# The next pair's token reads split from their layernorm, two weight reads on another queue, filler matmuls and differences placed earlier

## The chip, the cores and the metric

One core of one Trainium2 chip runs the kernel: a whole decoder layer, one launch. The metric is the device time in microseconds (us). The core's engines are called PE (TensorE, matrix products), DVE (VectorE), ACT (ScalarE), POOL (GpSimd) and SP (SyncE, which here only issues transfers). Each engine works through its own list of instructions in order.

## What is computed

Three stages, each with a residual, on 2 batches of 2048 tokens of width 512, all in float32:

```
x = x + linear_attention(layernorm(x))          # 16 heads of 32, 128 features
x = x + cross_attention(layernorm(x), ctx)      # 154 keys a batch, 16 heads
x = x + experts(layernorm(x))

def experts(h):                                 # h: 4096 tokens x 512
    scores = softmax(h @ router_w, axis=-1)     # 8 experts
    topk_w, topk_idx = top_k(scores, 6)
    f_all = (silu(h @ w_gate) * (h @ w_up)) @ w_down       # for each expert, 256 wide
    y = sum(picked(f_all, topk_idx) * topk_w)
    return y + (silu(h @ ws_gate) * (h @ ws_up)) @ ws_down # shared, 512 wide
```

## The kernel before

The tokens are cut into 8 blocks of 512, and a block into 4 tiles of 128 (NT). Linear attention takes the time to about 640 us, cross attention to about 1090 us, and the experts run from about 1042 us to the end. Every float32 product is made of three matmuls of rounded parts: an operand is split into a high part (a cast on ACT) and a low part (the subtraction `low`, L118, on DVE or POOL).

**The experts.** Blocks go in pairs: pair 0 (blocks 0 and 1) to pair 3. Each pair passes ten units: the 8 experts and the two halves of the shared product. That makes 40 steps, `todo3`, numbered n = 0 to 39; u is the unit in a pair. A unit's up and gate products for two blocks and two halves of the width are made by a scheme of seven products (NP = 7, as in Strassen's), the parts s = 0 to 6 of `products(n)` (matmuls `pg`, L1092). Their left operands `wq{n}_{j}` are made from the raw weights in pair 0 (`prepare`, from `rgu`, with `low` and with sums on POOL or DVE) and stored to DRAM as `wqs`; later pairs read them back. Their right operands `xo{g}_{s}` are the tokens of the pair and four differences of them, a to d: `token_difference` (L1054, on POOL for every pair but the first) and then `tokens_part`, which splits into high and low (cast L1067 and L118). The results are combined on DVE (L1106, L1109, L1112, L1124). The down products are plain in pair 0 (`down`: matmuls `pf` L148, then accumulated on DVE at L1285, scaled by the gate), and again by seven parts in later pairs (`down_products`: `pf` L1205 from `ht` and `hb`, summed on DVE at L1226; between the two POOL multiplies with the gate rows `gr` (L1155) and makes differences (L1165 to L1168)).

**The tokens of the next pair.** While units 1 to 7 of a pair run, `normalize_ahead(b, t)` reads one tile of the next pair's two blocks (`xsn`, 256 KB, L287), makes its layernorm (statistics L245, `mv_n` L248, on POOL two small operations L250 and L251, and the application L252) and stores it again, to `xn2`. It is recorded at part s == 3, one tile a unit, and in unit 5 another at s == 6. In unit 8 (`expert_ahead`) these tiles are read back (`xsf`), transposed on PE (`ptf`) and copied to `raws`; then `route` and what follows it make the gates, and `store_gates` writes them to DRAM (`gated`, two stores). For pair 0, `expert_ahead` makes the layernorm itself, during the last block of cross attention.

**Order.** Work is recorded by generators that wait in a list, `dense`; each step of it records one matmul, and `dense.after(n, do)` records a piece n matmuls later. What is recorded is then put in order, engine by engine, by a scheduler that runs when the program is built, with costs of its own. An instruction recorded with `tc.keep_in_program_order` (called `held` in the code) may not pass the one recorded before it on its engine. All matmuls are held, the differences on POOL too (L1054), and the layernorm's statistics where `normalize(..., pinned=True)` is called (L245); everything else may be moved by the scheduler, transfers included. `places` says at which part of a pair's last unit (keys 0 to 6) and of the next pair's first unit (7 and up, that is NP + s) the next pair's differences and operands are recorded: `places[0]` for the steps from pair 1 to 2 and from 2 to 3 (n = 19 to 20 and n = 29 to 30), `places[1]` for the step from pair 0 to 1.

**Buffers.** Prepared weights, operands and raw weights share 17 buffers of 8 KB a partition (`eight`); work tiles of 2 KB share 9 (`half`); the token tiles `xsn` and `xsf`, cross attention's residual rows `xr_x` and the gate rows `gr` share five (tag `xs`). PSUM has four banks for `ps` (`pg` among others) and four for `sc` (`pf`, `ptf`, `pto`, `pgt`).

**The last block of cross attention.** At its second step the layernorm of block 0 is recorded, and `load_unit(0)` reads unit 0's raw weights (`rgu0`, two transfers of 512 KB, and `rd0`, one) on SP's queue. At its tenth step the layernorm and the transposes of block 1 (`ln`, `tr`), the first two products of unit 0 (`ready[0]`, `ready[1]`) and the last two output products of block 6 (`outs[2]`, `outs[3]`: `cross_out`, 12 matmuls `po_x` each) are put in line.

Of the kernel before, what the change touches and what calls it, by code (L numbers as in the profile page):

```python
# [24 lines left out]
NT = TB // P  # L25
# [12 lines left out]
def decoder_layer(  # L38
# [26 lines left out]
    nc = tc.nc  # L65
# [26 lines left out]
    def chunked(w):  # L92
        return w.rearrange("(c p) n -> p c n", p=P)
# [124 lines left out]
    dense = Dense()  # L218
# [66 lines left out]
    def load_tile(d, b, t, name):  # L285
        xs = work.tile([P, D], F32, tag="xs", name=f"xs{name}{b}_{t}", bufs=5)
        nc.sync.dma_start(out=xs, in_=tile_of(d, b, t))  # L287
        return xs
# [30 lines left out]
    x2 = [dram.tile([TB, D], F32, name=f"x2_{b}") for b in range(nblk)]  # L319
# [4 lines left out]
    xs = [half(f"xs{t}") for t in range(NT)]  # L324
# [6 lines left out]
    raw = wk  # L331
    wk = [eight([P, NC, D], FR, f"wk_{i}") for i in ("hi", "lo")]
    for t in range(NT):
# [5 lines left out]
        b = nc.vector.tensor_tensor(lo, pt, hi.bitcast(F32), ALU.subtract)  # L339
# [427 lines left out]
    for s in range(ws_gate.shape[1] // F):  # L767
# [9 lines left out]
        out=before,  # L777
        in_=before,
# [3 lines left out]
        base=0,  # L782
        channel_multiplier=0,
    )
    accs, raws, gates = {}, {}, {}
    xn2 = {b: dram.tile([TB, D], F32, name=f"xn2_{b}") for b in range(GROUP, nblk)}

    def expert_ahead(b):
# [22 lines left out]

        return [values(t) for t in range(NT)], [turn(t) for t in range(NT)]

    def normalize_ahead(b, t):

        xs = normalize(load_tile(x2[b], 0, t, f"n{b}_"), f"n{b}_{t}")
        dense.after(8, lambda: nc.sync.dma_start(out=tile_of(xn2[b], 0, t), in_=xs))
        yield from ()

# [112 lines left out]
    def load_unit(n):  # L932
        if n >= len(units):
            return
        g, up, dn, _ = units[n]
        raw = eight([P, 2, NC, F], F32, f"rgu{n}")
        nc.sync.dma_start(out=raw[:, 0], in_=chunked(g))
        nc.sync.dma_start(out=raw[:, 1], in_=chunked(up))
        if n:
            rawd = late.tile([P, NF, D], F32, tag="rd", name=f"rd{n}", bufs=1)  # L940
        else:
            rawd = eight([P, NF, D], F32, f"rd{n}")
        nc.sync.dma_start(out=rawd, in_=chunked(dn))
        wraw[n] = raw, rawd

    def summed(a, b, op, name, shape, eager):
# [453 lines left out]
    for n in range(len(steps) + LAG + 1):  # L1400
        if n < len(steps):
            b, c, t = steps[n]
            k = NT * c + t
            dense.until(xsts, (b, c))
            scores(b, c, t)
            if b == 0:
                if k == 0:
                    load_values(0)
                if k in (NC - 1 + 0, NC + 1 + 0):
                    load_reciprocals(nblk - 1, k - 0 - NC + 1)  # L1410
                if NC + 0 <= k < 2 * NC + 0:
                    attended(nblk - 1, k - NC - 0)
                if k == 8:
                    bor = load_row(bo, "bor")
                    xwo = split_weight(wo_t, "xwo")
            if b == 0 and k == 0:
                ln, tr = layernorm(x1[1], 1, 0, qts, "x")
                outs = [[attention_out(nblk - i, t) for t in range(NT)] for i in (2, 1)]
                new = [cross_query(1, i) for i in range(NC)]
                kinds = {"L": ln, "a": outs[0], "T": tr, "b": outs[1], "q": new}  # L1420
                dense.add(*(kinds[x].pop(0) for x in "LLLaTLTaTTaaqbqbqbqb"))
            if k == LAG + 0 and b:
                outs = [cross_out(b - 1, i) for i in range(NT)]
                new = [cross_query(b + 1, i) for i in range(NC)]
                if b + 1 < nblk:
                    ln, tr = layernorm(x1[b + 1], b + 1, 0, qts, "x")
                    kinds = {"L": ln, "o": outs, "T": tr, "q": new}
                    dense.add(*(kinds[x].pop(0) for x in "LLLoTLTTToqoqoqq"))
                else:
                    dense.add(outs[0], tr[0], ln[3], outs[1], *tr[1:])  # L1430
            if b == nblk - 1 and k == 1:
                ln, tr = expert_ahead(0)
                dense.add(*ln[:3])
                load_unit(0)
            if b == nblk - 1 and k == 9:
                ln, tr = expert_ahead(1)
                ready = products(0)
                dense.add(prepare(0, 0), *ln[:3], tokens_part(0, 0), tokens_part(0, 1))
                dense.add(tr[0], ready[0], ln[3], *tr[1:], ready[1], *outs[2:])
            dense.fill(fl(k, 9.5 if b == 0 else 7.75 if b < nblk - 1 else 5.5))  # L1440
            if b % bpb == bpb - 1 and b + 1 < nblk and c > 0 and t == 1:
                load_keys(b // bpb + 1, c - 1)
            if b % bpb == 0 and b and k == 0:
                load_keys(b // bpb, NC - 1)
        if LAG <= n < len(steps) + LAG:
            turn(*steps[n - LAG])
        if n > LAG:
            b, c, t = steps[n - LAG - 1]
            if t == NT - 1:
                values(b, c)  # L1450
                if c == NC - 1 and (b + 1) % bpb == 0 and b + 1 < nblk:
                    load_values((b + 1) // bpb)
# [28 lines left out]
    def load_until(n, kind, j, more):  # L1481
# [12 lines left out]


    places = [
        {1: "0", 3: "a1", 4: "b", 5: "c2d", 7: "3", 8: "4", 9: "5", 10: "6"},
        {1: "0", 2: "1", 3: "abc2", 4: "d3", 5: "4", 6: "5", 7: "6"},
    ]
    MORE = 3  # L1500
    for n, (group, u) in enumerate(todo3):
        early_group = n < len(units)
        g = group[0]
        more = group[-1] + 1 < nblk
        ahead = [[], []]
        if u == len(units) - 2 and more:
            ahead = [expert_ahead(b) for b in range(group[-1] + 1, group[-1] + 3)]
        parts = products(n) if n else ready
        downs = [[] for _ in range(NP)]
        if n > len(units):  # L1510
            downs = [[d] for d in down_products(n - 1)]
        if u == 1 and n > len(units) + 1:
            f0, f1 = finished(g - GROUP, 0), finished(g - GROUP, 1)
            downs[0] = f0[:2] + downs[0] + f0[2:]
            downs[1] = f1[:2] + downs[1] + f1[2:]
        if n == LAST:
            f0, f1 = finished(g, 0), finished(g, 1)
            d = downs
            downs = [d[0], d[1], d[2], d[3] + d[4], d[5] + d[6], f0, f1]
        for s, part in enumerate(parts):  # L1520
            if not early_group:
                if s % 2 == 0:
                    dense.add(load_until(n, "w", s // 2, MORE))
            if n or s > 2:
                dense.add(part)
            if not early_group:
                if s in (0, 4):
                    dense.add(load_until(n, "d", s // 4, MORE))
                dense.add(*downs[s])
            if u == len(units) - 1 and more and s in places[early_group]:  # L1530
                dense.add(*tokens_parts(group[-1] + 1, places[early_group][s]))
            if u == 0 and n and NP + s in places[n == len(units)]:
                dense.add(*tokens_parts(g, places[n == len(units)][NP + s]))
            if not n and s == 0:
                dense.add(prepare(0, 2), *(tokens_part(0, i) for i in (4, 5, 6)), prepare(0, 3))
            if not n and s == 5:
                dense.add(down_sums(0))
            if s == 1 and n and n <= len(units):
                dense.add(down(n - 1, 1))
            if s == 1 and not n:  # L1540
                dense.add(load_accs(group))
            at = u - 1 if s == 3 else NT + 2 if s == 6 and u == 5 else -1
            at += s == 3 and u > 6
            if more and 0 <= at < GROUP * NT and u < len(units) - 2:
                dense.add(normalize_ahead(group[-1] + 1 + at // NT, at % NT))
            if ahead[0]:
                (ln, tr), (ln2, tr2) = ahead
                todo = (ln, [], tr[:2], tr[2:] + ln2, [], tr2[:2], tr2[2:])
                dense.add(*todo[s])
            if s % 2 and n + 1 < len(units):  # L1550
                dense.add(prepare(n + 1, s // 2))
            if s == 5 and n + 1 == len(units):
                dense.add(load_until(n + 1, "w", 0, MORE))
        if n + 1 < len(units):
            dense.add(prepare(n + 1, 3), down_sums(n + 1))
        if early_group:
            dense.add(down(n, 0))
        if not n:
            load_unit(1)
        dense.run()  # L1560
        load_gates(n + 1)
        load_unit(n + 2)
# [73 lines left out]
```

## Time and profile before

| | us |
|---|---|
| median of 3 runs | 2323.12 (2322.77 to 2324.95) |
| the profiled execution | 2323.05 |
| its span, first to last instruction | 2321.2 |
| mean granted TensorE clock | 0.988 |

The granted clock is the share of full speed that the chip's throttle let TensorE have.

Busy time of the engines by stage:

```profile
core 0: us, PE busy (x) PEld busy (x) DVE busy (x) ACT busy (x) POOL busy (x), PEclk, DMA share, GB/s
0.00:640.00 640.00, 602.59 (x3917) 434.30 (x3918) 383.16 (x603) 387.68 (x706) 308.05 (x298) 0.98 0.75 218
640.00:1042.00 402.00, 378.84 (x2439) 289.05 (x2439) 299.34 (x688) 274.71 (x1132) 234.22 (x243) 0.98 0.62 179
1042.00:1404.00 362.00, 349.09 (x1580) 273.39 (x1578) 285.40 (x398) 156.22 (x295) 206.64 (x173) 0.99 0.64 235
1404.00:1694.00 290.00, 289.46 (x1289) 235.89 (x1290) 224.05 (x335) 92.27 (x155) 145.95 (x117) 1.00 0.60 228
1694.00:1999.00 305.00, 301.97 (x1359) 245.91 (x1358) 245.52 (x361) 99.30 (x162) 169.42 (x131) 0.99 0.61 230
1999.00:2321.00 322.00, 314.82 (x1400) 255.54 (x1398) 244.05 (x353) 90.98 (x150) 164.18 (x119) 1.00 0.55 204
```

A row is a stretch of the span: its start and end, its length, and then for PE, PE's weight loads, DVE, ACT and POOL the busy time in us with the number of instructions; then the granted clock, the busy share of the 16 DMA engines and what they moved. The rows are linear attention, cross attention up to the first expert product, and pairs 0, 1, 2 and 3. In a timeline line, further on, the columns are start, busy time, engine, line, operation, the tiles (output <- inputs), shapes and count, and in brackets the idle time of the engine before it and what ended that. PE's busy time is from modelled ends of matmuls that overlap; a matmul of 512 columns counts 0.39 us alone, and one follows another after some 0.23 us.

### The profile page before, as it was taken

To read this page: it belongs to the slowest core of one execution; us is meant where nothing else is said; L and a number is where in the kernel's file an instruction comes from. 1 tells how busy PE (TensorE), PEld (TensorE's weight loads), DVE (VectorE), ACT (ScalarE), POOL (GpSimd) and SP (SyncE) were. 2 spreads that over 40 slices of the span, in tenths; PEclk is the share of its full clock that TensorE was granted. 3 is DMA by queue.
4 is the path that set the end of the run, shared out by engine and by line. 5 is a ranking of instruction groups with operands and counts; after the bars stand their busy time and mean duration, and the time that the engine had idled before them with its cause. 6 is when DMAs were issued, how large, how long until landed. Compare 5 with 4: busy or idle time off the path is not lost.

```text
span 2321.2 us, 35197 instructions
## 1 busy us (share of the span) xinstructions
PE 2236.8 (96%) x11978; PEld 1734.1 (75%) x11978; DVE 1681.5 (72%) x2733; ACT 1101.2 (47%) x2598; POOL 1228.5 (53%) x1078
## 2 busy tenths in 40 slices
PE   7999999989989999999999999999999999999999
PEld 5888777645667776766787877888878888788887
DVE  6554565568577777778977766788797887877777
ACT  4555677656566676765334343222433223432221
POOL 5445433546475565553855454555474554755443
PEclk9999999999999999999999999999999999999999
DMA  6555777899975565665866657565557656575553
GB/s 200 177 179 176 210 216 212 249 238 282 252 210 156 173 183 164 185 186 202 299 239 249 228 189 283 220 229 237 191 189 276 231 231 236 196 281 205 208 190 132
DMA packets 201809, 498.23 MB, mean 215 GB/s; under 512 B 27738, under 2 KB 47578, under 8 KB 181694
## 3 DMA queue, kind: packets, MB, share of 16 engines
q1 hardware_dynamic: 199902, 489.89, 63.4%
q0 software_dynamic: 1728, 6.09, 0.9%
q8 instruction: 96, 1.57, 0.3%
q14 instruction: 83, 0.68, 0.1%
HBM read 351.30 MB, written 144.60 MB: 214 GB/s over the span
## 4 chain that ended last, share of the span: by engine, by line
PE 73%; DMA 11%; DVE 7%; issue 3%; ACT 2%; POOL 2%; SPq 1%; DVEq 0%; ACTq 0%; POOLq 0%
PE pg L1092 28%; PE pf L1205 11%; PE pk L148 3%; PE pq L148 3%; PE pv L148 3%; PE pf L148 3%; PE po_x L148 3%; PE xpq L148 3%; PE pp L402 2%; PE pc L745 2%; PE psc L693 2%; PE xpt L725 2%; PE pkv L230 1%; PE po_a L148 1%; DMA wds<-wdq 1%
## 5 line engine op out<-in xcount | busy, mean ns | idle before, releaser
L1092 PE MATMUL pg<-xo,wq 128*128 128x512 f32 x3360 | 823.9, 392 | 4.3 <-DVE u L1106 1.5
L1092 PEld LDWEIGHTS pg<-xo,wq 128*128 128x128 f32 x3360 | 630.0, 188 | 144.7 <-DVE u L1106 2.8
L407 POOL TENSOR_TENSOR kacc<-kacc,e_k 128x512 f32<-128x512 f32 x128 | 166.0, 1298 | 225.1 <-DVE e_k L366 212.1
L1226 DVE TENSOR_TENSOR sum<-sum,pf 128x512 f32<-128x512 f32 x376 | 252.3, 683 | 45.1 <-PE pf L1205 41.0
L703 ACT ACTIVATE xe<-psc,nb 128x154 f32<-128x154 f32 x512 | 194.7, 413 | 91.6 <-DVE nb L700 86.7
L708 POOL TENSOR_TENSOR xe<-xe,sm 128x616 f32<-128x616 f32 x128 | 157.1, 1232 | 94.7 <-DVE sm L707 69.4
L1205 PE MATMUL pf<-ht,wdo 128*128 128x512 f32 x696 | 186.4, 394 | 4.4 <-DVE sum L1226 4.4
L1155 POOL TENSOR_TENSOR u<-u,gr 128x512 f32<-128x512 f32 x48 | 63.6, 1325 | 211.0 <-DVE u L1124 206.9
L366 DVE SCALAR_TENSOR_TENSOR e_k<-pp,e_k 128x512 f32<-128x512 f32 x128 | 87.5, 685 | 108.1 <-ACT e_k L365 102.7
L1205 PEld LDWEIGHTS pf<-ht,wdo 128*128 128x128 f32 x696 | 130.6, 189 | 34.8 <-DVE sum L1226 6.0
L1123 ACT ACTIVATE u<-u 128x512 f32<-128x512 f32 x80 | 50.6, 633 | 206.5 <-DVE u L1112 206.4
L1205 PE MATMUL pf<-hb,wdo 128*128 128x512 f32 x522 | 146.7, 397 | 0.0
L148 PE MATMUL pf<-wd,hp 128*128 128x512 f32 x528 | 134.0, 400 | 5.5 <-DVE mv_n L248 3.4
L148 PEld LDWEIGHTS pf<-wd,hp 128*128 128x128 f32 x528 | 99.4, 190 | 34.4 <-issue 6.5
L700 DVE TENSOR_REDUCE nb<-psc 128x2 f32<-128x308 f32 x256 | 111.5, 465 | 11.4 <-PE psc L693 11.3
L703 ACT ACTIVATION_READ_ACCUMULATOR xe<-psc,nb 128x1 f32 x512 | 117.1, 229 | 0.0
L1112 DVE TENSOR_TENSOR u<-u,pg 128x512 f32<-128x512 f32 x160 | 108.3, 681 | 11.1 <-PE pg L1092 9.9
L1205 PEld LDWEIGHTS pf<-hb,wdo 128*128 128x128 f32 x522 | 97.3, 188 | 23.0 <-DVE sum L1226 1.7
L364 ACT ACTIVATE e_k<-pp 128x512 f32<-128x512 f32 x128 | 76.8, 601 | 70.1 <-PE pp L402 62.5
L693 PE MATMUL psc<-xkst,xst 96*128 96x154 f32 x512 | 92.2, 287 | 12.5 <-ACT xe L703 8.6
L693 PEld LDWEIGHTS psc<-xkst,xst 96*128 96x128 f32 x512 | 78.0, 193 | 27.7 <-ACT xe L703 19.9
L402 PEld LDWEIGHTS pp<-pst,kst 96*128 96x128 f32 x512 | 75.9, 192 | 27.0 <-issue 10.5
(285 smaller groups left out, 5138.1 us busy)
## 6 DMA issues: line engine op xcount, KB each, us to landing
wq<-wqs SPq DMA_DIRECT2D x90, 1024.0 KB
wqs<-wq SPq DMA_DIRECT2D x30, 1024.0 KB
wdo<-wds SPq DMA_DIRECT2D x29, 1024.0 KB
kst<-kd SPq DMA_DIRECT2D x96, 256.0 KB
qst<-qd SPq DMA_DIRECT2D x96, 256.0 KB
xst<-xqd SPq DMA_DIRECT2D x96, 256.0 KB
wdo<-wds SPq DMA_DIRECT2D x29, 768.0 KB
kd<-khl SPq DMA_DIRECT2D x32, 512.0 KB
```

The lines of the kernel that those rows point to most:

```text
L148: nc.tensor.matmul(dst, lhsT=a, rhs=b, start=n == 0, stop=n == len(todo) - 1)
L366: nc.vector.scalar_tensor_tensor(e, src, 0.0, e, ALU.max, ALU.add)
L402: nc.tensor.matmul(pp[:, h], lhsT=stks[b, c][:, h, rows], rhs=pst[:, head], start=True, stop=True)
L407: nc.gpsimd.tensor_tensor(acc, acc, kp, ALU.add)
L693: nc.tensor.matmul(psc[:, i], lhsT=xsts[b, c][:, h, t * P : (t + 1) * P], rhs=ksts[bt, c][:, h, :], start=True, stop=True,)
L700: nc.vector.tensor_reduce(nb[:, two], psc, AX.X, ALU.max, negate=True)
L703: nc.scalar.activation(e[:, h, :], psc[:, i], AF.Exp, bias=nb[:, h : h + 1], accum_out=sm[:, h : h + 1],)
L708: nc.gpsimd.tensor_tensor(e, e, sm.unsqueeze(2).to_broadcast([P, 4, keys]), ALU.mult)
L1092: nc.tensor.matmul(pb, lhsT=w[:, p, i, k, :], rhs=xop[:, q, k, :], start=first and m == 0, stop=m == len(todo) - 1, skip_group_check=True,)
L1112: nc.vector.tensor_tensor(dst, dst, pb, ALU.add)
L1205: nc.tensor.matmul(banks[i], lhsT=w[:, p, i * P : (i + 1) * P], rhs=t[q], start=new and m == 0, stop=m == len(TERMS) - 1, skip_group_check ...
L1226: nc.vector.tensor_tensor(dst, dst, banks[i], ALU.add)
```

## The change

Four parts, in one diff.

1. The read of a token tile of the next pair and its layernorm are two pieces now: `load_ahead` (at s == 1, in unit 5 also at s == 4) and `normalize_ahead` (at s == 3, in unit 5 also at s == 6, as before). The layernorm is called with `pinned=True`, so that its statistics on DVE keep their place in the recorded order. The reads are not held.
2. `load_unit(0)` issues its three reads on POOL's queue (`nc.gpsimd`); the other units' stay on SP's.
3. In the last block of cross attention, `outs[2]` stands ahead of unit 0's first product and of block 1's transposes, and `outs[3]` ahead of its third and fourth, instead of both behind `ready[1]`.
4. `places[0]` has the differences a to d and the operands 1 and 2 one part sooner, operands 3 and 4 two parts sooner (in the last unit of the pair, no longer in the next pair's first), operand 5 where it was, and operand 6 one part later.

```
+    def load_ahead(b, t):
+        xsn[b, t] = load_tile(x2[b], 0, t, f"n{b}_")
+        yield from ()
+
     def normalize_ahead(b, t):
 
-        xs = normalize(load_tile(x2[b], 0, t, f"n{b}_"), f"n{b}_{t}")
+        xs = normalize(xsn.pop((b, t)), f"n{b}_{t}", pinned=True)
         dense.after(8, lambda: nc.sync.dma_start(out=tile_of(xn2[b], 0, t), in_=xs))
         yield from ()
...
         raw = eight([P, 2, NC, F], F32, f"rgu{n}")
-        nc.sync.dma_start(out=raw[:, 0], in_=chunked(g))
-        nc.sync.dma_start(out=raw[:, 1], in_=chunked(up))
+        queue = nc.sync if n else nc.gpsimd
+        queue.dma_start(out=raw[:, 0], in_=chunked(g))
+        queue.dma_start(out=raw[:, 1], in_=chunked(up))
...
-        nc.sync.dma_start(out=rawd, in_=chunked(dn))
+        queue.dma_start(out=rawd, in_=chunked(dn))
...
-                dense.add(tr[0], ready[0], ln[3], *tr[1:], ready[1], *outs[2:])
+                dense.add(outs[2], ready[0], tr[0], ln[3], tr[1], outs[3], ready[1], *tr[2:])
...
     places = [
-        {1: "0", 3: "a1", 4: "b", 5: "c2d", 7: "3", 8: "4", 9: "5", 10: "6"},
+        {1: "0", 2: "a1", 3: "b", 4: "cd2", 5: "3", 6: "4", 9: "5", 11: "6"},
         {1: "0", 2: "1", 3: "abc2", 4: "d3", 5: "4", 6: "5", 7: "6"},
     ]
...
-            at = u - 1 if s == 3 else NT + 2 if s == 6 and u == 5 else -1
-            at += s == 3 and u > 6
+            at = u - 1 if s in (1, 3) else NT + 2 if s in (4, 6) and u == 5 else -1
+            at += s in (1, 3) and u > 6
             if more and 0 <= at < GROUP * NT and u < len(units) - 2:
-                dense.add(normalize_ahead(group[-1] + 1 + at // NT, at % NT))
+                part = load_ahead if s in (1, 4) else normalize_ahead
+                dense.add(part(group[-1] + 1 + at // NT, at % NT))
```

More of the change, by code (lines that the diff above doesn't have):

```diff
@@ L784, in decoder_layer @@
     )
-    accs, raws, gates = {}, {}, {}
+    accs, raws, gates, xsn = {}, {}, {}, {}
     xn2 = {b: dram.tile([TB, D], F32, name=f"xn2_{b}") for b in range(GROUP, nblk)}
```

## The prediction

> **What bounds the kernel now.** I read the page's busy times and its chain first, then the windows, then the matmul engine's timeline at the few places where it stood still, and there the timelines of the engines that it waited for.
>
> ```profile
> PE 2236.8 (96%) x11978; PEld 1734.1 (75%) x11978; DVE 1681.5 (72%) x2733; ACT 1101.2 (47%) x2598; POOL 1228.5 (53%) x1078
> PE 73%; DMA 11%; DVE 7%; issue 3%; ACT 2%; POOL 2%; SPq 1%; DVEq 0%; ACTq 0%; POOLq 0%
> ```
>
> PE is the bound: 2236.8 of 2321.2 us. No matmul is added or removed, so the change can only win PE's idle time (and time at a reduced clock), or add to it. The windows say where that idle time is in the expert stage:
>
> ```profile
> core 0: us, PE busy (x) PEld busy (x) DVE busy (x) ACT busy (x) POOL busy (x), PEclk, DMA share, GB/s
> 1030.00:1060.00 30.00, 24.16 (x155) 18.18 (x154) 20.66 (x42) 19.15 (x64) 19.19 (x20) 0.89 0.46 149
> 1060.00:1105.00 45.00, 41.27 (x221) 30.03 (x220) 38.73 (x65) 24.17 (x52) 13.93 (x12) 1.00 0.67 244
> 1105.00:1130.00 25.00, 19.93 (x76) 14.76 (x75) 25.00 (x38) 9.96 (x17) 24.92 (x27) 0.93 0.79 289
> 1400.00:1410.00 10.00, 8.53 (x37) 6.45 (x36) 8.74 (x13) 4.61 (x7) 1.67 (x2) 1.00 1.01 423
> 1700.00:1725.00 25.00, 21.97 (x88) 16.94 (x87) 23.35 (x25) 8.84 (x13) 25.00 (x15) 0.93 0.73 260
> 2005.00:2030.00 25.00, 22.11 (x93) 16.91 (x92) 22.72 (x24) 8.40 (x12) 25.00 (x15) 1.00 0.73 273
> ```
>
> These are the start of the experts inside the last cross-attention block (call it A), the next 45 us (B), the first unit's down product (C), the step from pair 0 to pair 1 (E), from 1 to 2 (F), from 2 to 3 (G). Idle and reduced clock are two losses: at A PE idles 5.84 us, and a mean clock of 0.89 over 30 us is 3.3 us more at full rate; in C and F 0.93 over 25 us is 1.75 us each. At C the DVE column is full (25.00 of 25) and POOL's nearly so. The waits themselves:
>
> ```profile
> 1041.42 1.09 PE L805 MATMUL ptf<-ident,xsf 128*128 128x128 f32 x4 [4.26 <-DVE xsf L252]
> 1122.62 1.85 PE L148 MATMUL pf<-wd,hp 128*128 128x512 f32 x3 [3.42 <-DVE mv_n L248]
> 1401.26 0.70 DVE L245 BATCH_NORM_STATS2 st_n<-xsn 128x6 f32<-128x512 f32 x1 [2.23 <-DMA xsn<-x]
> 1713.19 1.51 PE L1205 MATMUL pf<-ht,wdo 128*128 128x512 f32 x3 [2.31 <-DVE sum L1226]
> 2017.14 0.95 PE L1205 MATMUL pf<-ht,wdo 128*128 128x512 f32 x3 [1.71 <-DVE sum L1226]
> L245 DVE BATCH_NORM_STATS2 st_n<-xsn x24: 654/692/696, 1101.0 to 1888.7; 128x6 f32<-128x512 f32 x24
> L252 DVE TENSOR_SCALAR xsn<-xsn,mv_n,rs_n x24: 532/874/1519, 1106.7 to 1896.4; 128x512 f32<-128x512 f32 x24
> ```
>
> The last two lines are durations in ns (shortest, median, longest) of the next pair's layernorm, 24 token tiles in three pairs. The sum below is made against the profiled execution: 2323.05 us, its span 2321.2 and 1.85 around it; the median of the runs, 2323.12, lies 0.07 above, so one number serves for both.
>
> **Part 1, reads apart from the layernorm, the statistics held.** Before, all eight normalizations of the first pair floated to 1101-1124: 8 x (0.692 + 0.17 for L248 + 0.874) = 13.9 us of DVE inside C's full column, ahead of the accumulates (L1285) that free the PSUM banks of `pf`. PE's 3.42 us wait is ended by a DVE count at L248. Held, the built order (the instructions of the changed kernel on each engine, which has no times) has one `st_n` behind each unit's third product from unit 1 on, none in unit 0. So C loses 13.9 us of DVE work against a wait of 3.42. POOL's 24.92 of 25 stays (it also loses 8 small pairs of 0.22 to 0.4 and 0.57 us), and 0.88 us of C's 1.24 other idle us are ended by ACT, so I take 3.42 and leave the 1.75 of clock as a reserve. **C: -3.4** (from -6.4, all idle and clock, to 0, POOL being the real owner).
> At E a held-up statistic stood in front of L118's differences: read issued at 1395.62, 5.62 us on the way, DVE stuck 2.23 us, PE idle 0.93 + 0.54. In the built order that statistic stands half a unit later. **E: -1.5** (to 0).
> The price: 13.9 us of DVE over units 1 to 7, 1.74 each in one of 30.9 us. Units of later pairs carry the same normalization already at DVE 46 to 48 and PE 58.0 us in windows of 58, so I take 0. If a held statistic's read is late, everything behind it on DVE waits (the next subtractions L1106 to L1124, which free PE's banks). Read and statistic are now two products apart, 2 x 30.9/7 = 8.8 us, against 5.62 on the way: 3.2 us of cover. Only the statistics are held; the reads still float, and share five buffers. The read's issue and its store's move on SP with the tile; gate rows for units 16, 17, 26 and 27 fall behind such stores, and still stand some 9 us ahead of their use. Without the cover it costs what E shows, 1.47 idle, and a loss of clock as at C, 1.75: 3.2 us a unit. **Units 1 to 7: 0** (to 22.5, seven times).
>
> **Part 2, unit 0's weights from POOL.** SP loses 0.41 + 2.09 + 0.51 = 3.0 us of issue at 1015-1018; POOL, idle from 1016.88 to 1019.02 there, gains three of 0.55 to 0.78 (its issues of other 512 KB and 1 MB tiles). ACT first casts these weights at 1036.60, 18.8 us after SP's last issue; POOL's 1 MB reads land 10.5 us after theirs. Hidden: **0**. Without that idle time the two `xe` products behind it on POOL come some 2 us later, and PE's `xpt` with them (0 to +2).
>
> **Part 3, two output products of block 6 as filler.** `outs[2]` and `outs[3]`, twelve matmuls of 0.23 us each (first to last start 1064.27 to 1066.89), move ahead of the transposes that wait at A. The 4.26 us gap is DVE's: reads of block 1's tiles land at 1036.4 to 1038.8 and their layernorm, not held, keeps its place. So 12 x 0.23 = 2.8 us of that wait are filled; the rest, 1.5, stays, with 1.5 at 1045.98 and 1047.73. Where they come from PE has 3.4 us of gaps of its own (1060 to 1075), of which their leaving may open more: I leave the clock's 3.3 us as the reserve for that. **A and B: -2.8** (from -9.1 to +1.7, half of the 3.4 again).
>
> **Part 4, differences sooner at F and G.** POOL now runs a, b, c, d (2.4 us each) back to back and ends some 7 us before the 1706.64 of before. That brings the casts and L118 at 1710.04, which stood in front of `sum` (L1226), forward by more than the 2.31 us that PE waits; `st_n`, 0.68 us at 1711.87 in the same place, leaves too (part 1). **F: -2.3 idle, -1.75 clock; G: -1.7.** What it adds: more buffers are alive, and in the built order weights `wq20_1` (and `wq30_1`) are issued behind the two gate stores, which waited until 1698.56 and 1699.98, not at 1688.01. Issued at 1700.3 and 8.08 us on the way (the read at 1703.77, next to others), they land by 1708.4; their first matmul is 39 matmuls x 0.23 = 9 us behind the one at 1697.6, at 1706.5. That is up to 1.9 late; a read nearly alone takes less, so +1.0 at each. **F: -3.05** (-4.8 to +3.65, late with 1.75 of clock), **G: -0.7** (-2.7 to +3.65).
>
> Here a rule speaks against part of this. The rows say that 2.31 us of idle cost clock (F, 0.93) and 1.71 did not (G, 1.00). The Trainium skill, "TensorE: Matmul & The Clock Gate", section "What's actually happening", has the clock fall only after an idle window of about 3.4 us. By it F would have no clock to win, and the forecast would be 1.75 higher, 2313.3; I keep to F's row.
>
> **The sum:** -3.4 - 1.5 + 0 + 0 - 2.8 - 3.05 - 0.7 = -11.45, so 2323.05 - 11.45 = **2311.6 us**.
>
> **The rivals.** (1) *The waits change hands.* C is POOL's as much as DVE's (24.92 of 25), A is the layernorm's, F and G trade the difference for weights that land late (each gain undone by its +1.9). For it: both columns are full at C. Against: the DVE events that end three of the five waits above. Then E (-1.5) and half of C (-1.7) are left: **2319.9**, no change that can be told.
> (2) *Held statistics wait for their reads* in units 1 to 7: slower. For it: E's line; reads float in SP's queue behind weight stores, and five buffers are freed by stores. Against: 3.2 us of cover, and 12 such waits, 14.6 us in all, of which only E's shows on PE. All seven: 2311.6 + 22.5 = **2334.1**. It decides from 11.45 / 3.2 = 3.6 units on.
> (3) *The change doesn't do what it says:* statistics stay bunched, C and E stay: 2311.6 + 4.9 = **2316.5**. The built order of DVE speaks against it.
>
> **How the numbers follow.** Forecast 0.60, rival 1 0.19, rival 2 0.18, rival 3 0.03. A measurement tells 0.2% (4.6 us) from no change: below 2318.5 is faster (forecast and rival 3, 0.63), above 2327.8 slower (rival 2, 0.18), between the same (rival 1, 0.19). All best ends together give 2323.05 - 9.1 - 6.4 - 1.5 - 4.8 - 2.7 = 2298.6, unlikely at once; I take 2302 below. Above, the range takes in rival 1 and the start of rival 2, to 2328. The forecast's own range is 2304 to 2318.
>
> **What would show it.** Right: no `st_n` in 1101-1124, DVE below 25 there and the 3.42 us gap gone; one `st_n` a unit without a DMA wait; the 4.26 us gap below 2; L118's fourth difference ahead of 1705 at F, PE's 2.31 gone. Wrong: PE waiting for `wq20_1` or `wq30_1`; DVE idle at `st_n` in units 1 to 7 with PE gaps after it; new gaps at 1060-1080 where the filler was taken from.

## The result and the profile after

| | before | the changed kernel |
|---|---|---|
| median of 22 runs, us | 2322.36 (2317.19 to 2329.89) | 2326.8 (2321.28 to 2335.21) |
| profiled execution, us | 2323.05 | 2330.45 (span 2328.7, clock 0.982) |

The ratio on record is 1.0024, 95% interval 1.0014 to 1.0034: slower by 0.24%, some 5.6 us (the two medians lie 4.4 us apart). The forecast was 11.45 us faster. The profiled execution lies 3.65 us above its median (2330.45 against 2326.8); the experiments show how far single executions differ.

Page of the changed kernel: busy times, the chain of waits by engine and by line.

```profile
PE 2239.6 (96%) x11978; PEld 1738.3 (75%) x11978; DVE 1681.9 (72%) x2733; ACT 1101.4 (47%) x2598; POOL 1229.0 (53%) x1081
...
PE 70%; DMA 11%; DVE 7%; POOL 5%; issue 3%; ACT 3%; SPq 1%; ACTq 0%; POOLq 0%; DVEq 0%
PE pg L1097 27%; PE pf L1210 12%; PE pk L148 3%; PE pq L148 3%; PE pv L148 3%; PE po_x L148 3%; PE xpq L148 2%; PE pf L148 2%; PE pp L402 2%; PE psc L693 2%; PE pc L745 1%; PE pkv L230 1%; PE xpt L725 1%; PE po_a L148 1%; POOL s L957 1%
```

(Code lines below the change have moved by 4 or 5: `pg` L1092 is now L1097, L1124 is L1129.) PE's share of the chain fell from 73 to 70%, POOL's rose from 2 to 5, and a POOL line that was not among the named ones before is: L957, the sums that make the next unit's weights. The windows say where:

```profile
core 0: us, PE busy (x) PEld busy (x) DVE busy (x) ACT busy (x) POOL busy (x), PEclk, DMA share, GB/s
1030.00:1060.00 30.00, 26.30 (x155) 19.69 (x154) 21.94 (x47) 19.37 (x68) 17.33 (x20) 0.83 0.48 156
1060.00:1105.00 45.00, 42.76 (x224) 30.57 (x224) 38.47 (x58) 25.03 (x48) 16.16 (x13) 0.96 0.66 237
1105.00:1130.00 25.00, 21.95 (x85) 17.38 (x84) 19.47 (x24) 9.06 (x16) 17.82 (x15) 0.86 0.73 262
1130.00:1360.00 230.00, 221.01 (x940) 176.52 (x939) 184.99 (x235) 84.28 (x144) 129.94 (x115) 0.99 0.66 240
1690.00:1725.00 35.00, 30.30 (x123) 23.64 (x123) 34.33 (x40) 13.62 (x20) 28.39 (x15) 0.90 0.41 155
1995.00:2030.00 35.00, 32.78 (x148) 26.31 (x147) 33.56 (x45) 14.33 (x21) 28.56 (x16) 1.00 0.48 169
```

The row that the prediction does not show, the first pair's units 1 to 8, in the kernel before:

```profile
1130.00:1360.00 230.00, 228.39 (x1003) 184.96 (x1002) 176.63 (x228) 89.73 (x154) 130.52 (x108) 1.00 0.67 246
```

PE idles 230 - 228.39 = 1.61 us there before and 8.99 after. At A and B idle time fell (30 - 24.16 to 30 - 26.30, and 3.73 to 2.24), but the clock did too (0.89 to 0.83, 1.00 to 0.96). At C (1105 to 1130) DVE has room now, 19.47 of 25 in place of 25.00, and PE still waits: idle time fell from 5.07 to 3.05, and the clock from 0.93 to 0.86.

**Idle time and clock over all runs.** The profile is one execution, and its clock of 0.982 is among the lowest of the changed kernel's runs (0.981 to 0.988). Every run has its clock on record. In the mean it is 0.9845 for the 22 runs of the changed kernel, and 0.9863 to 0.9872 for the kernel before in the four sets of 29 to 35 runs that the experiments below were compared with; on one chip, after_on_sync (the changed kernel without part 2) has 0.9843 against 0.9863. An estimate from these numbers: the span times the clock, which is what a run would take at full clock if PE were its bound throughout, comes to 2289.7 us for the changed kernel and to 2289.2 to 2290.7 for the kernel before. So at full clock the two are about equally long. In the profile the change wins idle time at A, B and C (14.64 us down to 8.99) and loses it in units 1 to 8 (7.38 us) and at F (1.67, further on). What is left of the loss is clock: the share that was not granted comes to 36.1 us of the span in the mean, in place of 29.6 to 31.9.

### The profile page after: what moved, and what is told of

Same layout as the page of the kernel before. It is cut to its first block, busy times and chain, and to the rows that moved or that the text cites. A ratio compares the mean times of both kernels' runs of the same rounds, so it can differ in the third digit from the quotient of the medians.

```text
span 2328.7 us, 35192 instructions
## 1 busy us (share of the span) xinstructions
PE 2239.6 (96%) x11978; PEld 1738.3 (75%) x11978; DVE 1681.9 (72%) x2733; ACT 1101.4 (47%) x2598; POOL 1229.0 (53%) x1081
## 4 chain that ended last, share of the span: by engine, by line
PE 70%; DMA 11%; DVE 7%; POOL 5%; issue 3%; ACT 3%; SPq 1%; ACTq 0%; POOLq 0%; DVEq 0%
PE pg L1097 27%; PE pf L1210 12%; PE pk L148 3%; PE pq L148 3%; PE pv L148 3%; PE po_x L148 3%; PE xpq L148 2%; PE pf L148 2%; PE pp L402 2%; PE psc L693 2%; PE pc L745 1%; PE pkv L230 1%; PE xpt L725 1%; PE po_a L148 1%; POOL s L957 1%
## 5 line engine op out<-in xcount | busy, mean ns | idle before, releaser
L1097 PE MATMUL pg<-xo,wq 128*128 128x512 f32 x3360 | 829.7, 394 | 10.3 <-ACT s L1108 8.8
L1097 PEld LDWEIGHTS pg<-xo,wq 128*128 128x128 f32 x3360 | 631.6, 189 | 151.7 <-ACT s L1108 11.9
```

The costliest lines, as they stand in the source:

```text
L1097: nc.tensor.matmul(pb, lhsT=w[:, p, i, k, :], rhs=xop[:, q, k, :], start=first and m == 0, stop=m == len(todo) - 1, skip_group_check=True,)
```

## Where the waits went

**Units 1 to 8.** Five waits of one kind, 1.42 to 2.38 us, each at a unit's end. One of them in the timelines of POOL, ACT and PE:

```profile
1212.31 3.02 POOL L118 TENSOR_TENSOR hp<-u,hp 128x512 fp32r<-128x512 f32 x2 [2.94 <-ACT hp L1134]
1215.29 1.30 POOL L957 TENSOR_TENSOR s<-rgu,s 128x512 f32<-128x512 f32 x1
...
1216.62 0.62 ACT L992 CAST wq<-s 128x512 fp32r<-128x512 f32 x1 [3.51 <-POOL s L957]
1217.15 1.07 ACT L1108 COPY s<-pg 128x512 f32<-128x512 f32 x2
...
1217.78 1.43 PE L1097 MATMUL pg<-xo,wq 128*128 128x512 f32 x5 [1.43 <-ACT s L1108]
```

The last hidden parts `hp` of a unit are split late; their two low parts (3.0 us on POOL) stand ahead of the sum `s4` for the next unit's last weights; ACT's cast of that sum stands ahead of its copy of the next unit's first product; and PE may not add the second product to that bank before the copy is made. Nothing in that chain is the layernorm, and nothing in it waits for a read. The same chain before, one unit later:

```profile
1246.03 0.62 ACT L987 CAST wq<-s 128x512 fp32r<-128x512 f32 x1 [2.66 <-POOL s L952]
...
1247.19 1.19 PE L1092 MATMUL pg<-xo,wq 128*128 128x512 f32 x4 [0.24 <-ACT s L1103]
```

PE already waited there, for 0.24 us: the chain had no slack left, and a row with 228.39 us busy of 230 doesn't show that.

**C.** DVE and PE at unit 0's down product, first in the kernel before, then in the changed one:

```profile
1116.33 0.68 DVE L118 TENSOR_TENSOR hp<-s,hp 128x512 fp32r<-128x512 f32 x1
1116.93 1.51 DVE L252 TENSOR_SCALAR xsn<-xsn,mv_n,rs_n 128x512 f32<-128x512 f32 x1
1118.37 0.68 DVE L245 BATCH_NORM_STATS2 st_n<-xsn 128x6 f32<-128x512 f32 x1
1118.97 1.17 DVE L118 TENSOR_TENSOR wdq<-ds,wdq 128x512 fp32r<-128x512 f32 x1
1120.06 1.74 DVE L118 TENSOR_TENSOR wq<-rgu,wq 128x512 fp32r<-128x512 f32 x1
1121.73 0.74 DVE L1285 SCALAR_TENSOR_TENSOR acc<-pf,gates,acc 128x512 f32<-128x512 f32 x1
1122.39 0.17 DVE L248 BATCH_NORM_AGGREGATE mv_n<-st_n 128x2 f32<-128x6 f32 x1
```

```profile
1112.50 1.77 DVE L118 TENSOR_TENSOR wq<-rgu,wq 128x512 fp32r<-128x512 f32 x1
1114.19 2.28 DVE L118 TENSOR_TENSOR wd<-rd,wd 128x1024 fp32r<-128x1024 f32 x1
1116.40 1.40 DVE L1290 SCALAR_TENSOR_TENSOR acc<-pf,gates,acc 128x512 f32<-128x512 f32 x2
...
1117.28 2.90 PE L148 MATMUL pf<-wd,hp 128*128 128x512 f32 x6 [3.05 <-DVE acc L1290]
```

Before, the last work ahead of the first accumulate was 2.2 us of layernorm and 2.9 us of low parts. The layernorms have left, and the low part of `wd` for unit 1 (2.28 us), which stood behind the accumulate at 1124.43 before, has moved up into their place.

**F.** ACT, DVE and PE at the step to pair 2:

```profile
1703.88 0.62 ACT L1153 CAST hb<-s 128x512 fp32r<-128x512 f32 x1 [2.03 <-PE pf L1210]
1707.81 0.62 ACT L1153 CAST hb<-u 128x512 fp32r<-128x512 f32 x1 [3.31 <-DVE xo L118]
1708.33 1.05 ACT L906 COPY gt<-pgt 8x512 f32<-8x512 f32 x2
...
1706.51 1.21 DVE L118 TENSOR_TENSOR xo<-t,xo 128x1024 fp32r<-128x1024 f32 x1
...
1708.95 2.00 PE L1210 MATMUL pf<-hb,wdo 128*128 128x512 f32 x6 [3.91 <-ACT gt L906]
```

The cast into `hb` gets the buffer of the temporary difference (`t2`, one of the four of tag `hl`), and has to wait until DVE's low part of operand 2 has read that. The two copies of the gates stand behind the cast on ACT, and PE, out of `sc` banks, behind the copies. The differences themselves are sooner: the fourth ends 1706.03 - 1703.05 = 3.0 us behind the start of the second gate transposes, against 1706.64 - 1697.19 = 9.5 before.

**A.** The longest wait now stands before the attention's own transposes `xpt`, and is one for DVE's copy of the attention's scores:

```profile
1041.73 1.97 PE L725 MATMUL xpt<-ident,xe 128*128 128x128 f32 x8 [2.59 <-DVE att L732]
```

## The experiments

Each ratio is to the kernel before, run on the same chip. Two columns are worked out from each run's profile: PE's idle time from 1130 to 1360, and the stretch from ACT's 21st cast of cross attention's output (`cx`) to its first copy of a product in step n = 11, which holds A, B, C, units 1 to 9 and E. The first column is the time of that cast. The idle time repeats from profile to profile, the stretch less well. In the changed kernel and in after_gates_sooner PE, DVE, ACT and POOL do the same work in the same order from the cast to about 1380 us, and their stretches are 498.9 and 490.5: in the first PE has half clock for 27.3 us of it, in the second for 10.2.

| run | that cast at, us | stretch, us | idle 1130 to 1360, us | ratio, 95% interval |
|---|---|---|---|---|
| before | 944.0 | 490.0 | 1.61 | |
| control_before | 941.5 | 488.2 | 1.27 | 1.0004 (0.9990 to 1.0018) |
| the changed kernel | 941.3 | 498.9 | 8.99 | 1.0024 (1.0014 to 1.0034) |
| part1_alone | 949.3 | 494.6 | 8.82 | 1.0040 (1.0025 to 1.0054) |
| part1_reads_only | 943.4 | 489.2 | 1.51 | 1.0003 (0.9989 to 1.0017) |
| part1_no_norm | 945.7 | 491.4 | 5.91 | 0.9999 (0.9990 to 1.0008) |
| part1_sum_sooner | 941.0 | 491.3 | 6.97 | 1.0007 (0.9997 to 1.0016) |
| part2_alone | 947.2 | 489.8 | 1.43 | 1.0019 (1.0006 to 1.0032) |
| part2_again | 949.7 | 490.1 | 1.05 | 1.0008 (0.9999 to 1.0017) |
| part3_alone | 937.2 | 491.2 | 1.74 | 1.0001 (0.9988 to 1.0013) |
| part4_alone | 943.9 | 489.9 | 2.06 | 1.0002 (0.9992 to 1.0011) |
| after_on_sync | 945.1 | 493.5 | 8.58 | 1.0015 (1.0001 to 1.0029) |
| after_sum_sooner | 940.9 | 492.7 | 7.72 | 1.0003 (0.9991 to 1.0016) |
| after_weights_later | 940.6 | 486.5 | 8.33 | 1.0006 (0.9995 to 1.0017) |
| after_gates_sooner | 937.5 | 490.5 | 9.58 | 1.0013 (1.0000 to 1.0026) |
| before_sum_sooner | 944.6 | 485.6 | 0.00 | 0.9978 (0.9966 to 0.9989) |
| best_sum_weights | 944.9 | 483.2 | 0.00 | 0.9983 (0.9972 to 0.9995) |
| best_all | 947.6 | 485.9 | 0.00 | 0.9987 (0.9978 to 0.9996) |

### The four parts alone, and the kernel before once more

Each part of the diff was put on the kernel before by itself (the hunks are those shown with the change).

> Before plus part 1 only (reads apart from the layernorm, statistics held). Theory (unit ends): with the statistics held, the order of the first pair's units changes so that at a unit's end POOL's two low parts of hp, then the sum s4, then ACT's cast of it stand in front of ACT's copy of the next unit's first product, and TensorE waits 1.4 to 2.4 us at five of the nine steps: +6 to +12 us against before, with those gaps before pg in 1140 to 1350. Rival (no part's own): any edit reshuffles the built order, part 1 alone is within 2 us of before and the five gaps are not there.

> Before plus part 4 only (differences and operands sooner). Theory: at the step from pair 1 to 2 ACT stands at the cast into hb, whose buffer is that of the third difference, until DVE's low part of operand 2 has read it; the gates' copies are behind it and TensorE waits 3 to 4 us in place of 2.3: +1 to +4 us over both steps. Rival (the prediction's): the differences end sooner and the steps win 2 to 4 us, -2 to -4.

> Before plus part 3 only (two output products of block 6 as filler). Theory: the 4.26 us wait shrinks to about 2.6 and gaps at 1060 to 1075 stay: -1 to -3 us. Rival: the filler's work is only moved and the clock stays low longer: 0 to +2.

> Before plus part 2 only (unit 0's weights on POOL's queue). Theory: hidden, within 1.5 us of before. Rival: POOL's three issues push the last block's products on POOL and its exponentials: +1 to +3.

Part 1 carries the loss: 1.0040, with the same five gaps (1.25 to 2.39 us) as in the changed kernel. The 1.0040 is from 7 runs and may be high: of the 7.9 us by which the span in its profile is longer than before's, 5.3 lie ahead of the cast, where nothing was changed. Its window:

```profile
1130.00:1360.00 230.00, 221.18 (x943) 176.89 (x942) 187.59 (x238) 83.06 (x142) 130.02 (x115) 0.99 0.67 242
```

Part 4 alone changes nothing that can be measured: F waits 2.22 us for the gates' copy in place of 2.31 for the sum, and both steps get 0.95 of the clock in windows of 35 us, where only F had it before. Part 3 alone neither: its filler takes the wait at A from 4.26 to 1.50 and 1.27, and the wait at C grows to this:

```profile
1116.20 2.04 PE L148 MATMUL pf<-wd,hp 128*128 128x512 f32 x4 [5.58 <-DVE acc L1285]
```

Part 2 alone came out 0.19% slower, but from the 21st cast on its profile runs as before does (489.8 against 490.0). Ahead of that cast no instruction is in another place in any of these kernels. So the kernel before was run as its own control, and part 2 once more:

> Before itself, unchanged, as a measure of what such a comparison can tell. Every theory: ratio 1.000 within its interval, the profiled span from the cross attention's 21st cast of its output (cx) to the end 1377 us within 1.5. If it is off by as much as part 2 alone (+0.19%), part 2's loss is no loss of its own; if not, part 2 costs something ahead of the part of the program that it changes.

> Part 2 alone once more, to tell its +0.19% from chance. If its loss is real: ratio above 1.0010 again. If it was chance (the control's 1.0004 and a profile that ends as before from cross attention's 21st cast on): ratio within 0.9985 to 1.0010, profiled time from that cast 1377 us.

The control was 1.0004; the second run of part 2 gave 1.0008, inside the bound set for chance. The column of casts says what such intervals hold: 937.2 to 949.7 us for the same instructions in the same order. One execution can't tell 0.2%. In the kernels that have before's order on PE the stretch behind the cast differs by less, 488.2 to 490.1 in six profiles. Part 2 was also taken out of the changed kernel:

```
-        queue = nc.sync if n else nc.gpsimd
+        queue = nc.sync
```

> The changed kernel without part 2 (unit 0's weights on SP's queue again). If part 2 costs 3 to 4 us in the whole too: 2323 or below. If it is hidden: 2326 to 2328, as the changed kernel.

1.0015 against 1.0024, intervals that overlap. The whole times don't settle a price of part 2; behind the cast, its two profiles run as before does.

### Part 1: the reads or the held statistics

```
-        xs = normalize(xsn.pop((b, t)), f"n{b}_{t}", pinned=True)
+        xs = normalize(xsn.pop((b, t)), f"n{b}_{t}")
```

> Before plus the reads of part 1 recorded apart and sooner, with the statistics not held. Theory (holding them is what costs): within 2 us of before, statistics again bunched at the first down product, no gaps of 1.4 us before pg at the unit ends. Rival (the reads' place costs, by SP's queue and the five buffers): slower by the 9 us of part 1 alone.

The run tells more than was asked. In its trace every engine, SP with its transfers too, works in the order of the kernel before, by line and tile: the scheduler put the reads back where they had been (the first issued at 1091.61, before at 1092.66). So it is one more run of the kernel before (stretch 489.2, idle 1.51, ratio 1.0003). All that part 1 does, its loss too, comes in with the holding of the statistics. What it would cost to issue the reads sooner without the hold is not shown.

### Part 1: the order at the unit's end, or the added work

First the order: the last weights of the next unit are recorded in the sixth part, ahead of what makes `hp`.

```
             if s % 2 and n + 1 < len(units):
                 dense.add(prepare(n + 1, s // 2))
+            if s == 5 and n + 1 < len(units):
+                dense.add(prepare(n + 1, 3))
...
-            dense.add(prepare(n + 1, 3), down_sums(n + 1))
+            dense.add(down_sums(n + 1))
```

> Part 1 alone, with the last weights of the next unit (its sum s4 on POOL, cast and low part) recorded in the sixth part of a unit rather than behind the seventh, so that the sum stands ahead of the two low parts of hp on POOL. Theory (the chain hp low, s4, cast, copy of the first product is what TensorE waits for): the five gaps of 1.3 to 2.4 us go, 6 to 10 us faster than part 1 alone, at or below before. Rival (DVE's added 1.74 us a unit is what delays, whatever the order on POOL): gaps stay, within 2 us of part 1 alone.

> The changed kernel with the same sum recorded sooner. Theory: the five gaps at unit ends go, together 8.7 us of idle and about 3.4 of reduced clock: 2318 or below, faster than before by 4 to 8 us; the wait of 3.9 us at the step from pair 1 to 2 stays. Rival: as above, no gain over the changed kernel (2327).

Then the work: the tiles of pair 1 stored as they were read, without the layernorm.

```
-        xs = normalize(xsn.pop((b, t)), f"n{b}_{t}", pinned=True)
+        xs = xsn.pop((b, t))
+        if b >= 2 * GROUP:
+            normalize(xs, f"n{b}_{t}", pinned=True)
```

> Part 1 alone, but the tiles of pair 1 are stored as read, without their layernorm (left out: 8 layernorms, 13.9 us of DVE and small POOL work in units 1 to 7). On POOL the sum s4 still stands behind the two low parts of hp. Theory A (the order is what costs): gaps of 1 to 2 us at the unit ends stay, time near part 1 alone (2329 to 2332). Theory B (DVE's and POOL's added work delays the chain that ends in the sum): the gaps shrink below 0.5, 6 to 10 us faster than part 1 alone (2321 to 2325).

Both bring the time back: 1.0040 falls to 1.0007 with the sum sooner, and to 0.9999 without the layernorms, and the changed kernel's 1.0024 to 1.0003. That doesn't show that either of them is the cause. The next experiment has the sum sooner win as much where no statistic is held, so its gain is one of its own. And idle time doesn't follow: without the layernorms 5.91 us of it are left, against 1.61 before. A chain without slack, which is late when DVE has 1.74 us more to do in the unit and earlier when the sum doesn't wait for `hp`, agrees with both, but it is an argument. Neither clears all the gaps. Without the layernorms two of 1.3 to 1.4 us stay; with the sum sooner the waits before `pg` are mostly replaced by waits of 0.8 to 1.4 us before `pf`:

```profile
1130.00:1360.00 230.00, 223.03 (x969) 178.65 (x968) 194.03 (x242) 87.32 (x151) 149.60 (x119) 1.00 0.67 246
```

Here DVE has 194.03 us of work in 230, against 176.63 in the kernel before. The theory's gaps were to go, and idle time went by a fifth only, from 8.82 to 6.97; the stretch is 3.3 us shorter (494.6 to 491.3). The 8 us between the two medians are more than that, and the difference is left open. A scheduler that sees fewer operations orders all the others anew, so the second test changes the order too, and no exact split between work and order is shown.

### The kernel before with the sum sooner

The same edit of the recording order on the kernel before.

> Before with the next unit's last weights recorded in the sixth part. Theory: before has only two small gaps at unit ends (1.2 us in all), so 0 to -2 us; if the gain of 8 us seen with part 1 were the sum's place alone, whatever the statistics do, -4 or more.

```profile
1130.00:1360.00 230.00, 230.00 (x1016) 187.71 (x1015) 187.24 (x231) 90.18 (x155) 143.18 (x106) 1.00 0.68 248
```

Not one idle moment of PE is left in these 230 us, and the ratio is 0.9978 (0.9966 to 0.9989), 7 runs. The theory's 0 to -2 us was wrong: the medians lie 4.7 us apart, which is what the expectation has for a gain of the sum's place alone, whatever the statistics do. Only 1.61 us of it can be idle time of this window; the stretch is 4.4 us shorter (490.0 to 485.6), and where the rest of that comes from was not followed up.

### C: who owns the wait at the first down product

The changed kernel with unit 1's last weights recorded behind unit 0's down product, and the low parts of two of them held there:

```
-            if s % 2 and n + 1 < len(units):
+            if s % 2 and n + 1 < len(units) and (n or s < 5):
...
-            dense.add(prepare(n + 1, 3), down_sums(n + 1))
+            if n:
+                dense.add(prepare(n + 1, 3), down_sums(n + 1))
         if early_group:
             dense.add(down(n, 0))
+        if not n:
+            dense.add(prepare(1, 2), prepare(1, 3), down_sums(1))
...
+                if n == 1 and j == 2 and not o:
+                    held(ins)
...
+            if n == 1:
+                held(ins)
```

> The changed kernel with unit 1's weights 4 to 6 (wq1_2, wd1, wq1_3) recorded behind unit 0's first down product, and the low parts of wq1_2 and wd1 held there on DVE, so that the four accumulates of that product stand ahead of them. Theory (low parts of 1.8 and 2.3 us ahead of the accumulates own the wait): the 3.05 us wait falls below 1 and its reduced clock with it, 2 to 5 us faster than the changed kernel, 2322 to 2325. Rival (POOL, which is full there): the wait moves to hp's low part or to the sum, within 1.5 us of the changed kernel.

The accumulates stand together now, and the wait is gone. DVE and PE:

```profile
1109.13 2.73 DVE L1294 SCALAR_TENSOR_TENSOR acc<-pf,gates,acc 128x512 f32<-128x512 f32 x4 [0.28 <-PE pf L148]
...
1107.53 8.56 PE L148 MATMUL pf<-wd,hp 128*128 128x512 f32 x36
```

36 matmuls run without a break. In the changed kernel the low parts of the weights own this wait: the layernorms had left before, and DVE, as the timeline above has it, went from one low part to the next without idling. (The edit also moves POOL's sums for these weights, so POOL was not tested apart.) The time goes the same way, 1.0006 (0.9995 to 1.0017) in place of 1.0024 (1.0014 to 1.0034), though the intervals touch; the waits at unit ends are still there (idle 8.33).

### F and G: the gates' copies

```
-                    dense.after(14 + 14 * j, lambda at=b + j: store_gates(at))
+                    dense.after(8 + 14 * j, lambda at=b + j: store_gates(at))
```

> The changed kernel with the gates' transposes and copies recorded six matmuls sooner, so that on ACT both copies stand ahead of the casts into hb. Theory (ACT stands at hb for the third difference's buffer with the copies behind it): the waits of 3.9 and 2.2 us fall below 2 and 1.5, 2 to 5 us faster than the changed kernel, 2322 to 2325. Rival (DVE, slowed beside POOL's four differences, is late with everything): the wait goes to sum or to the next product, no gain.

In the built order both copies stand ahead of the casts into `hb` now, and the trace has ACT make them at 1688.30. The wait for them is gone from PE's timeline; three others stand there:

```profile
1700.26 0.74 PE L1210 MATMUL pf<-hb,wdo 128*128 128x512 f32 x2 [1.05 <-DVE hb L118]
...
1706.22 1.20 PE L1210 MATMUL pf<-ht,wdo 128*128 128x512 f32 x4 [0.93 <-ACT ht L1153]
...
1712.76 1.62 PE L1097 MATMUL pg<-xo,wq 128*128 128x512 f32 x6 [2.14 <-ACT ht L1153]
```

4.12 us together against 4.70. So the copy behind `hb` was a real wait, and taking it away shows the next ones, DVE's low part of `hb` and ACT's casts of `ht`: the rival is right that the wait only moves. The time, 1.0013, can't be told from the changed kernel's.

### Together

best_sum_weights is the kernel before with the sum sooner and unit 1's weights later; best_all has part 4 and the gates' copies sooner on top.

> Before with the sum sooner (which alone gave 0.9978) and unit 1's weights later, held as in after_weights_later. Theory: the two gains add, 3.4 us of wait and 1.7 of clock at the first down product on top: ratio 0.995 to 0.9965, 2311 to 2316. If the wait moves only: 0.9975 as with the sum alone.

> The same with part 4 (differences sooner) and the gates' copies sooner. Theory: another 2 to 5 us at the steps to pairs 2 and 3: ratio 0.993 to 0.996. If part 4 has no gain even so: as best_sum_weights within 1.5 us.

0.9983 and 0.9987 can't be told from the 0.9978 of the sum alone; the expected 0.9965 or less wasn't reached. In the profiles the stretch is shortest with both edits (483.2, against 485.6 with the sum alone). The wait at C is halved to 1.75 us and not gone: the layernorms are still bunched there, and DVE has them ahead of the accumulates. So at C any work that stands there owns the wait, low parts or layernorm. All three are faster than both kernels of the comparison, by some 3 to 5 us against before.

## Why the prediction was wrong, step by step

The sum holds -9.7 us of idle time and, at F, -1.75 of clock. By the estimate from all runs the time at full clock did not change, and the clock took some 4 to 6.5 us more than before. The steps follow with their idle time; where a step's clock is given, it is that of the one profile.

**"Units 1 to 7: 0".** This is the step that failed. The cover named for it, later pairs that carry the same layernorm at PE 58.0 of 58, was taken from units of another kind: there the weights come back from DRAM, while in pair 0 DVE, POOL and ACT also make them (sums, casts, low parts), and the chain that makes the last of them ends at PE. The price was 7.4 us more of idle time (1.61 to 8.99); in every profile with the statistics held 7.0 to 9.6 us of idle time stand there. In the changed kernel's profile two of the waits, 2.38 and 2.10 us, were followed by half clock (0.99 over these 230 us). In after_gates_sooner the same waits were not:

```profile
1130.00:1360.00 230.00, 220.42 (x960) 175.98 (x959) 186.32 (x239) 91.33 (x157) 131.12 (x116) 1.00 0.67 246
```

So this part of the price differs from run to run, and only the mean clock of the runs says what all the waits cost together. The rival that stood on the right place, held statistics in units 1 to 7, had the wrong mechanism: no statistic waits for its read in the changed kernel. The view of `st_n` there, with no line under its idle time:

```profile
L245 DVE BATCH_NORM_STATS2 st_n<-xsn x24: 682/687/689, 1131.9 to 1937.1; 128x6 f32<-128x512 f32 x24
...
its engine sat idle before it (us, times) until:
who waited for it (us, times):
```

**"C: -3.4".** Wrong owner. The releaser named in the profile, a count at L248 of 0.17 us (1122.39), only came last: the accumulate that frees a bank stands right ahead of it (1121.73), and ahead of that two low parts. Of the 13.9 us of layernorm 8.8 stood inside C, and 6.4 of these ahead of that accumulate; two of the eight statistics came behind it. (C's other idle time was 5.07 - 3.42 = 1.65 us, not 1.24.) All of the layernorm left, the wait stayed at 3.05 us, and C's idle time fell by 2.0 us. The clock over C was 0.86, 3.5 us against 1.75, in this profile. The reading that would have shown it: list all that stands on DVE between the last finished `pf` bank and its accumulate, not the last of it.

**"E: -1.5".** The statistic left, and PE waits 1.33 us there for a low part of an operand in place of 1.47: no gain.

**"A and B: -2.8".** Idle time fell by 2.1 and 1.5 us, more than the sum's 2.8, but in this profile the clock took 1.8 back at each. Alone, part 3 moved nothing in the time, as rival 1 has it for this step.

**"F: -3.05, G: -0.7".** The gain on the differences is there (6.5 us sooner against the gate transposes). The new wait was looked for on SP's queue, at `wq20_1`, and stood on ACT, at a buffer that `t2` and `hb` share. F idles 4.70 us in place of 3.03, with 3.5 us of clock in place of 1.75 in this profile; G 2.22 in place of 2.90 (1995 to 2030). `wq20_1` is issued at 1709.78, 9.5 us later than worked out, behind the gates as expected, and nothing waits for it: PE itself is late.

**Part 2: 0.** Not contradicted, and not settled by the whole times. **Rival 3** is out: the statistics stand one to a unit, from 1131.9 on.

The step behind all of this is one in the description of the kernel before: it says that all matmuls are held. Only those of the linear attention that are recorded at L230 (`pkv`, `pn`) are; the expert matmuls are placed by the scheduler, as the casts and copies are. Without the hold part 1 leaves every engine's order as it was (part1_reads_only); with it PE, DVE, ACT and POOL all have another one in the first pair. An order's gains and losses can't be read from the 24 small operations that were held.

## What to carry to other kernels

Before adding work to a stage that shows no idle time, follow the chain that ends at each of its joints and measure its slack there: here there was none, PE already waited 0.24 us, while the engine that got the work was three quarters busy. Cover is taken from a stage that does the same work, not from one that looks like it. A wait's named releaser is the last of a queue: what owns the wait is everything that stands there between the data being ready and the operation that frees the buffer. And one profile shows which waits are there; what they cost in clock takes the mean of many runs.

## What the runs showed of the hardware

**The same program, the same order, 1.3% apart.** The part of the program ahead of the change took 937.2 to 949.7 us over 18 profiled executions. In the profiles, the time at half clock in it differs from one to the next, from 10 to 16 stretches of 3.41 us.

**The clock doesn't follow from a wait's length alone.** The wait of 2.3 us at F was followed by half clock in the kernel before (0.95 over 35 us) and not in best_sum_weights (1.00). Of the waits at unit ends, those of 2.38 and 2.10 us in the changed kernel were (0.94 from 1145 to 1175, 0.93 from 1275 to 1300), and the same two in after_gates_sooner, 2.39 and 1.92 us, were not (1.00 from 1135 to 1165 and from 1265 to 1290). Waits of 1.4 us at the unit ends were followed by it in neither. The Trainium skill, "TensorE: Matmul & The Clock Gate", section "What's actually happening", has the window free-running, which agrees; its idle window of about 3.4 us is more than these rows needed.

**DVE beside POOL.** In the changed kernel the product of two 128x512 tiles at L1129 (`u<-u,u`) takes 0.691 us in the median and 2.43 at most, at 1695.19, beside one of POOL's differences that part 4 moved there. The Trainium skill, "SBUF — State Buffer", section "Who interferes with whom", says that an operation of VectorE with two inputs in SBUF contends with one of GpSimd that reads SBUF. The rows agree. In the kernel before the longest such product took 1.81 us, so this is not new, but it falls in a worse place: two more of these products, of 1.65 and 2.09 us (1702.15 and 1704.49), stand ahead of the low part for which the cast into `hb` waits at F. The prediction left this out; what it costs was not measured apart.
